# Keys, values and the last element's Wh in tiles of 512 positions, projected block by block

## The chip, the cores and the metric

The kernel runs on one core of a Trainium2 chip. The time is the device time of one execution in microseconds (us); beside it the profile gives the span from the first to the last instruction. TensorE (PE) multiplies matrices, VectorE (DVE), ScalarE (ACT) and GpSimd (POOL) work on tiles, and SyncE (SP) issues all the DMAs of this kernel, in program order.

## What is computed

Two layers on a graph of N = 2048 nodes, for a batch of 8 elements with 256 features:

```python
# layer 0: attention of 4 heads (D = 64), softmax within chunks of 256 keys, the chunks summed
q, k, v = (x @ W.T + b for W, b in ((Wq, bq), (Wk, bk), (Wv, bv)))
s = clip(q @ k.T / 8, -10, 10); s = where(adj == 0, -10, s)
ctx = sum over chunks j of softmax(s[:, chunk j]) @ v[chunk j]
h = layernorm(x + layernorm(ctx @ Wo.T + bo + x) * gamma + beta)
# layer 1: graph attention
Wh = h @ W; si = Wh @ a[:256]; sj = Wh @ a[256:]
e = where(adj > 0 or i == j, leaky_relu(si[:, None] + sj[None, :], 0.2), -inf)
out = layernorm(h + elu(softmax(e) @ Wh))
```

`adj` is the same for all elements. All arithmetic is float32.

## The kernel before

**Order by hand.** The order of instructions is the program's own; each engine takes its instructions in that order, and the framework adds the waits. The main loop (from L749) runs over J, the pairs of key tiles: 8 elements x 4 query blocks of 512 (`IB`) x 8 chunks of 256 keys, and each J has two halves. A half is a *beat*: one tile of 128 keys against 512 queries, all heads. There are 512 beats with scores, 64 per element and 16 per query block; `2 * total` in the code is beat 512. After it a drain loop (L868) runs beats without scores.

**A beat.** `begin_beat` advances layer 1's pipeline of an earlier element (`low` on ScalarE L611, `leaky` L615 and `edges` L620 on VectorE, `weights` on ScalarE L624). Then come the scores (L775, TensorE), the clip and mask in one VectorE instruction (L785), the exponentials (L788, ScalarE), and the products of the exponentials of the previous J with the values and with ones (L801, TensorE). Sums go out to a DMA (`dc`, L817), are inverted (L823), stored (`rd`, L825) and spread over the partitions (`r`, L829); two beats later `un` is scaled (L836) and added to `ctxT` by GpSimd (L837). `end_beat` does layer 1's products with Wh (L643, and L658 for the last element), then advances generators one step each: `ahead` (the preludes of layer 1) and `fins` (the end of layer 0 for a query block, `fin`; of layer 1, `fin1`; and the making of masks). After beat 512 `fins` goes first.

**Keys and values.** They lie in one tile each per element: `kT` (2 x 2048 per partition) and `v` (16 x 256), both from a pool of one buffer (`one`). `make_kT` projects four blocks of 512 (L252, evicted by ScalarE L253) in one go: for element 0 before the main loop, for the others at the last beat of the element before, behind `make_qT`. `make_v` (L270, L277) follows after the first two beats of an element. Both load the transposed input, `xT` tiles of 512 KB from a pool of four, anew for keys and for values (`xT_k`, `xT_v`); the query block has its own load (`xT_q`). Accumulators of projections, ctx products, transposes and Wh share the PSUM pool `ps_m`, two buffers with the tag `m`.

**Masks of element 0.** The first mask block (`first_m0`) is made in four pieces of VectorE L154 and ScalarE L161 ahead of the loop; `masks_made` makes the other one of each pair and the later blocks, `far_made` the row masks `far`, both during element 0.

**Layer 1's prelude.** `prelude` multiplies h with W (`wh_block`, L370, L371), takes the key columns (`key_columns`, L380 to L382), turns them into a row on every partition (`key_rows`, L388 to L393), and finds each query's largest allowed sum with 32 maxima over half rows (`half_max`, L412), for which `far` is loaded into two buffers `fb`. `last_prelude` does it for element 7 when no scores are left to hide it: its `wh` takes the place of `kT`, and `sj_row` that of `v`, both from beat 512 on. The first half rows need Wh blocks 0 and 1; three first-half maxima are issued in each beat until `hT`, the transposed h of the last query block, is there (made by `fin`, L352 to L359, at beat 520: output projection L331 with its add L338 and statistics at 515, normalization L303 at 516, GpSimd L343 and L344 at 517, statistics at 518, normalization at 519). Then follow the last Wh block and the second half rows. Eight rows of `far` are held whole in the places of the exponentials.

The parts that the diff touches, and what calls them:

## Time and profile before

| | us |
|---|---|
| median of 3 runs | 4439.85 (4435.65 to 4445.19) |
| the profiled execution, its own time | 4440.12 |
| its span | 4438.3 |
| TensorE busy | 4076.7 (92%) |
| VectorE busy | 3412.6 (77%) |
| ScalarE busy | 2604.1 (59%) |
| GpSimd busy | 1782.7 (40%) |
| one key-tile score instruction of VectorE (L785), mean | 1.221 |
| one exponential (L788), mean | 1.022 |

A profile line names the line of the kernel, the engine, the operation, the tile that is written and those that are read (`sc<-qT,kT`), the form, and how many; in a timeline the first two numbers are the start and the length in us, and brackets hold the idle time of the engine just before, with what ended it. "PEld" is TensorE's loading of weights, which overlaps its matmuls. A projected block of keys is 8 matmul rows in the trace, of values 16. Of the whole span, the profile's chain of waits is only followed back for a part; the stages are therefore read from the busy time of each engine in a stretch.

### The profile page before, as it was taken

What the parts mean: (1) busy time and instruction counts of PE and PEld (TensorE: products, weight loads), DVE (VectorE), ACT (ScalarE), POOL (GpSimd) and SP (SyncE); (2) the same over time, 40 slices, a digit from 0 to 9 for tenths busy, and PEclk for the clock granted to TensorE, in tenths of its full rate; (3) what the DMA queues carried; (4) which work ended last, traced back from release to release, by engine and by line L of the source; (5) the groups of instructions that cost most, each with busy time, mean ns of one, the idle gap of its engine ahead of it and who ended that gap; (6) DMA issues with size and microseconds to landing.
All of it is one profiled execution on the core that took longest, in us unless ns stands there. A gap on an engine that the chain in (4) does not pass through costs nothing. (4 is left out here: it accounts for less than half of the span.)

```text
span 4438.3 us, 61328 instructions
## 1 busy us (share of the span) xinstructions
PE 4076.7 (92%) x23053; PEld 1913.9 (43%) x23053; DVE 3412.6 (77%) x4530; ACT 2604.1 (59%) x3878; POOL 1782.7 (40%) x906
## 2 busy tenths in 40 slices
PE   7888999999899999999989999999989999899767
PEld 3222334444344443445434453444534445344455
DVE  4776468985799758996599966898569975898786
ACT  4666456665556655666556655566555665566455
POOL 0222224553255523554334543455325543355521
PEclk9999999999999999999999999999999999999889
DMA  4555333322322323223333223332332232332321
GB/s 145 165 161 154 93 104 102 96 89 82 102 84 90 100 67 113 86 79 95 93 92 101 82 75 106 97 105 74 90 105 83 92 96 75 109 94 78 117 79 53
DMA packets 266601, 432.93 MB, mean 98 GB/s; under 512 B 85952, under 2 KB 121024, under 8 KB 265408
## 3 DMA queue, kind: packets, MB, share of 16 engines
q1 hardware_dynamic: 266304, 429.01, 31.5%
q8 instruction: 181, 2.97, 0.3%
q14 instruction: 116, 0.95, 0.1%
HBM read 357.96 MB, written 68.88 MB: 96 GB/s over the span
## 5 line engine op out<-in xcount | busy, mean ns | idle before, releaser
L788 ACT ACTIVATE e<-sc 128x1024 f32<-128x1024 f32 x1024 | 1037.3, 1022 | 1144.9 <-DVE sc L785 1100.5
L785 DVE SCALAR_TENSOR_TENSOR sc<-sc,mk 128x1024 f32<-128x1024 f32 x1024 | 1205.5, 1221 | 519.6 <-PE sc L775 287.1
L775 PE MATMUL sc<-qT,kT 64*128 64x512 f32 x4096 | 1063.6, 633 | 108.6 <-ACT e L788 105.9
L837 POOL TENSOR_TENSOR ctxT<-ctxT,un 128x1024 f32<-128x1024 f32 x224 | 564.9, 2522 | 1173.6 <-DVE un L836 1068.1
L801 PE MATMUL u<-e,v 128*32 128x512 f32 x8192 | 982.5, 597 | 0.0
L643 PE MATMUL us<-wh,w 128*128 128x256 f32 x3584 | 875.9, 393 | 74.3 <-ACT w L624 56.6
L643 PEld LDWEIGHTS us<-wh,w 128*128 128x128 f32 x3584 | 663.9, 192 | 416.6 <-ACT w L624 110.6
L633 POOL TENSOR_TENSOR acc<-acc,w 128x512 f32<-128x512 f32 x392 | 607.8, 1551 | 528.6 <-ACT w L624 512.7
L775 PEld LDWEIGHTS sc<-qT,kT 64*128 64x128 f32 x4096 | 347.5, 189 | 631.3 <-ACT e L788 310.8
L615 DVE SCALAR_TENSOR_TENSOR w<-ab,sj,w 128x512 f32<-128x512 f32 x512 | 587.6, 1168 | 15.4 <-ACT w L611 15.3
L801 PEld LDWEIGHTS u<-e,v 128*32 128x32 f32 x8192 | 240.3, 110 | 660.2 <-issue 539.6
L620 DVE TENSOR_TENSOR w<-w,mk 128x512 f32<-128x512 f32 x512 | 467.8, 934 | 42.9 <-DMA mk<-mask 40.0
L801 PE MATMUL u<-e,ones 128*32 128x512 f32 x4096 | 497.8, 604 | 0.0
L412 DVE CUSTOM_DVE_ANT_0 fb<-sj_row,fb 128x1024 bf16<-128x1024 f32 x240 | 383.8, 1608 | 2.4 <-DMA fb<-far 2.4
L611 ACT ACTIVATE w<-ab,sj 128x512 f32<-128x512 f32 x512 | 353.7, 716 | 18.0 <-PE us L658 11.9
L624 ACT ACTIVATE w<-w 128x512 f32<-128x512 f32 x512 | 310.5, 631 | 66.3 <-DVE w L620 64.9
L836 DVE TENSOR_TENSOR un<-un,r 128x1024 f32<-128x1024 f32 x224 | 278.8, 1244 | 88.2 <-DMA r<-rd 72.7
L809 ACT COPY un<-u 128x512 f32<-128x512 f32 x512 | 300.6, 587 | 54.8 <-PE u L801 52.9
L801 PEld LDWEIGHTS u<-e,ones 128*32 128x32 f32 x4096 | 107.7, 110 | 357.3 <-issue 315.7
L823 DVE RECIPROCAL dc<-dc 128x16 f32<-128x16 f32 x256 | 64.1, 250 | 180.3 <-DMA dc<-ds 155.2
L573 POOL TENSOR_TENSOR hx<-hx,hr 128x1024 f32<-128x1024 f32 x32 | 91.6, 2862 | 177.8 <-DVE hx L572 177.8
L658 PE MATMUL us<-wh,w 128*128 128x257 f32 x512 | 127.6, 412 | 28.8 <-ACT w L624 28.8
(100 smaller groups left out, 3163.1 us busy)
## 6 DMA issues: line engine op xcount, KB each, us to landing
r<-rd SPq DMA_DIRECT2D x256, 256.0 KB
mk<-mask SPq DMA_DIRECT2D x120, 512.0 KB
fb<-far SPq DMA_DIRECT2D x240, 256.0 KB
xT_k<-in_xT_dram SPq DMA_DIRECT2D x32, 512.0 KB
raw<-in_adjT_dram SPq DMA_DIRECT2D x32, 512.0 KB
xT_q<-in_xT_dram SPq DMA_DIRECT2D x32, 512.0 KB
rawf<-in_adj_dram SPq DMA_DIRECT2D x32, 512.0 KB
xT_v<-in_xT_dram SPq DMA_DIRECT2D x32, 512.0 KB
```

The costliest lines, as they stand in the source:

```text
L412: nc.vector.tensor_tensor_reduce(out=fb, in0=sj_row[:, ts(hf, HN)], in1=fb, scale=1.0, scalar=2 * FAR * 0.999, op0=ALU.add, op1=ALU.max, a ...
L611: nc.scalar.activation(self.w, k["ab"][:, 1, :], AF.Identity, bias=k["sj"][:, 1, c : c + 1])
L615: nc.vector.scalar_tensor_tensor(self.w, k["ab"][:, 0, :], k["sj"][:, 0, c : c + 1], self.w, ALU.add, ALU.max)
L620: nc.vector.tensor_tensor(self.w, self.w, self.k["mks"][self.c // HT][:, self.c % HT, :], ALU.min)
L624: nc.scalar.activation(self.w, self.w, AF.Exp)
L633: nc.gpsimd.tensor_add(k["acc"], k["acc"], self.w)
L643: nc.tensor.matmul(k["us"][:, t, :], self.w[:, ts(t, P)], k["wh"][:, c, 0:F], start=(first and t % 2 == 0), stop=last, skip_group_check=True,)
L775: nc.tensor.matmul(sc[:, h, :], kT[h * D : (h + 1) * D, hp, ts(c, P)], qT[h * D : (h + 1) * D, hp, :], start=True, stop=True,)
L785: nc.vector.scalar_tensor_tensor(scs[hp], scs[hp], -CLIP, cap, ALU.max, ALU.min)
L788: nc.scalar.activation(e, scs[hp], AF.Exp)
L801: nc.tensor.matmul(m[h * DH : (h + 1) * DH, :], prev["v"][:, pc, f0 : f0 + DH] if part < 2 else ones[:, 0:DH], prev["es"][2 * i + h // 2][ ...
L837: nc.gpsimd.tensor_add(p["ctxT"], p["ctxT"], p["un"])
```

## The change

Keys and values of an element become four tiles each, with buffers of their own (`kT0` to `kT3`, `v0` to `v3`). A generator, `projections`, projects block n of keys and, a beat or two later, block n of values, from the same `xT` tile. For element b > 0 that is at beats 4n + 4 and 4n + 5 of the last query block of element b - 1, when the old block n has had its last use. In element 0 key block 0 is made ahead of the loop, and the query block from the same `xT`; value block 0 at beat 0; key blocks at beats 2, 6, 10, and value blocks at 4, 8, 12. The first mask block is made one piece ahead of the loop and three in beats 0 to 2; the first loads are reordered to suit.

In the last element Wh block n (n = 0 to 2) goes into the place of `kT` n, at beats 502, 506 and 510, and its key columns with it; the first half row goes into the place of `v0`. One first-half maximum is issued per beat from beat 511 on, with every row mask from the two `fb` buffers; the second-half row masks, two rows to a tile, are the ones held in the places of the exponentials. Layer 1 reads Wh as a list of four tiles.

```diff
@@ -122,7 +122,7 @@
         return t
 
     WT = {"k": load_w("k", WkT)}
-    first_xT = [xT_tile(0, ib, "k") for ib in range(2)]
+    xT_kv = {(0, 0): xT_tile(0, 0, "k")}
     WT["q"] = load_w("q", WqT)
     bk_c = load_c("bk_c", bk)
     bq_c = load_c("bq_c", bq)

...
@@ -176,13 +176,16 @@
                     blocks0[ib, hf] = m0
                 m1 = two.tile([P, HT, IB], I8, tag="mask1", name=f"mb1_{ib}_{hf}")
                 for i in range(HT // 2 + 2):
-                    if i < HT // 2 and not first:
+                    if first:
+                        if 0 < i < HT // 2:
+                            make_mask(0, m0, raw, ib, hf, 2 * i, 2)
+                    elif i < HT // 2:
                         load_raw(raw, ib, hf, 2 * i, 2)
                     if i >= 2:
                         if not first:
                             make_mask(0, m0, raw, ib, hf, 2 * i - 4, 2)
                         make_mask(1, m1, raw, ib, hf, 2 * i - 4, 2)
-                    if i >= 2 or not first:
+                    if i or not first:
                         yield
                 nc.sync.dma_start(out=mask[0][ib, hf], in_=m0)
                 nc.sync.dma_start(out=mask[1][ib, hf], in_=m1)

...
@@ -204,10 +207,12 @@
                 yield
 
     first_raw = one.tile([P, HT, IB], I32, tag="wh", name="raw0_0")
-    for i in range(0, HT, 2):
-        load_raw(first_raw, 0, 0, i, 2)
-    first_xT.append(xT_tile(0, 2, "k"))
+    load_raw(first_raw, 0, 0, 0, 2)
     WT["v"] = load_w("v", WvT)
+    load_raw(first_raw, 0, 0, 2, 2)
+    xT_kv[0, 1] = xT_tile(0, 1, "k")
+    load_raw(first_raw, 0, 0, 4, 2)
+    load_raw(first_raw, 0, 0, 6, 2)
     WT["o"] = load_w("o", WoT)
     bv_c = load_c("bv_c", bv)
 

...
@@ -252,32 +257,52 @@
                 nc.tensor.matmul(pm, WT[name][:, k, ts(o, P)], xt[:, k, :], start=(k == 0), stop=(k == KC - 1))
             nc.scalar.activation(dst[:, o, :], pm, AF.Identity, bias=bias[:, o : o + 1], scale=scale)
 
-    def make_kT(b, tiles):
-        kT = one.tile([P, NPAIR, N], F32, tag="kT", name=f"kT{b}")
-        for ib in range(NIB):
-            proj_T(kT[:, :, ts(ib, IB)], "k", tiles[ib], bk_c, 1.0, f"k{b}_{ib}")
-            if len(tiles) < NIB:
-                tiles.append(xT_tile(b, len(tiles), "k"))
-        return kT
-
-    def make_v(b, tiles):
-        v = one.tile([P, NT, F], F32, tag="v", name=f"v{b}")
-        for ib in range(NIB):
-            for t2 in range(TPB // 2):
-                pv = ps_m.tile([P, 2, F], F32, tag="m", name=f"pv{b}_{ib}_{t2}")
-                for j in range(2):
-                    for k in range(KC):
-                        nc.tensor.matmul(
-                            pv[:, j, :],
-                            tiles[ib][:, k, ts(2 * t2 + j, P)],
-                            WT["v"][:, k, :],
-                            start=(k == 0),
-                            stop=(k == KC - 1),
-                        )
-                nc.scalar.copy(v[:, ib * TPB + 2 * t2 : ib * TPB + 2 * t2 + 2, :], pv)
-            if len(tiles) < NIB:
-                tiles.append(xT_tile(b, len(tiles), "v"))
-        return v
+
+
+    kTs = [[None] * NIB for _ in range(B)]
+    vs = [[None] * NIB for _ in range(B)]
+
+    def make_kT(b, n):
+        kTs[b][n] = one.tile([P, NPAIR, IB], F32, tag=f"kT{n}", name=f"kT{b}_{n}")
+        proj_T(kTs[b][n], "k", xT_kv[b, n], bk_c, 1.0, f"k{b}_{n}")
+
+    def make_v(b, n):
+        xt = xT_kv.pop((b, n))
+        vs[b][n] = one.tile([P, TPB, F], F32, tag=f"v{n}", name=f"v{b}_{n}")
+        for t2 in range(TPB // 2):
+            pv = ps_m.tile([P, 2, F], F32, tag="m", name=f"pv{b}_{n}_{t2}")
+            for j in range(2):
+                for k in range(KC):
+                    nc.tensor.matmul(
+                        pv[:, j, :],
+                        xt[:, k, ts(2 * t2 + j, P)],
+                        WT["v"][:, k, :],
+                        start=(k == 0),
+                        stop=(k == KC - 1),
+                    )
+            nc.scalar.copy(vs[b][n][:, ts(t2, 2), :], pv)
+
+    def projections():
+
+
+        for b in range(B):
+            first = (b * NIB - 1) * 2 * NCH
+            for n in range(NIB):
+
+
+                k_beat = 4 * n - 2 if b == 0 else first + 4 * n + 4
+                while beat < k_beat - 2:
+                    yield
+                if (b, n) not in xT_kv:
+                    xT_kv[b, n] = xT_tile(b, n, "k")
+                while beat < k_beat:
+                    yield
+                if (b, n) != (0, 0):
+                    make_kT(b, n)
+                    yield
+                while beat < k_beat + 2 and b == 0:
+                    yield
+                make_v(b, n)
 
     def make_qT(b, ib, xt):
         qT = one.tile([P, NPAIR, IB], F32, tag="qT", name=f"qT{b}_{ib}")

...
@@ -493,48 +517,54 @@
 
 
         st = states[b]
-        while beat < 2 * total - 4 or fin_near[b] < NIB - 1:
-            yield
-        hts = [load_hT(b, ib) for ib in range(NIB - 1)]
-        while beat < 2 * total:
-            yield
-        wh = one.tile([P, NT, F + 2], F32, tag="kT", name=f"wh{b}")
-        sj = two.tile([P, 3, NT], F32, tag="sj", name=f"sj{b}")
-        wh_block(b, wh, hts[0], 0)
-        yield
-        wh_block(b, wh, hts[1], 1)
+        wh, rows = [None] * NIB, [None] * 2
         halves = [slice(0, HT), slice(HT, NT)]
-        key_columns(wh, sj, halves[0])
-        yield
-        sj_row = one.tile([P, N], F32, tag="v", name=f"sj_row{b}")
-        key_rows(b, sj, sj_row, halves[0])
-        wh_block(b, wh, hts[2], 2)
-
-        held = []
-        for it in range(HT):
-            fr = eight.tile([P, N], BF16, tag="e", name=f"far{b}_{it}")
-            nc.sync.dma_start(out=fr.rearrange("p (n w) -> p n w", n=2), in_=far[it].rearrange("n p w -> p n w"))
-            held.append(fr)
-        fbs, fb_load = far_loads(b, [(it, hf) for hf in range(2) for it in range(HT, NT)])
-        yield
+        sj = None
+        for ib in range(NIB - 1):
+
+            while fin_near[b] <= ib or beat < 2 * total - 12 + 4 * ib:
+                yield
+            ht = load_hT(b, ib)
+            yield
+            yield
+            wh[ib] = one.tile([P, TPB, F + 2], F32, tag=f"kT{ib}", name=f"wh{b}_{ib}")
+            wh_block(b, wh[ib], ht, ib)
+            if sj is None:
+                sj = two.tile([P, 3, NT], F32, tag="sj", name=f"sj{b}")
+            key_columns(wh[ib], sj, slice(ib * TPB, (ib + 1) * TPB))
+            nc.vector.memset(wh[ib][:, :, F : F + 1], 1.0)
+            yield
+            if ib == 1:
+                rows[0] = one.tile([P, HN], F32, tag="v0", name=f"sj_row{b}_0")
+                key_rows(b, sj, rows[0], halves[0])
+                fbs, fb_load = far_loads(b, [(it, 0) for it in range(NT)])
         m2 = one.tile([P, NIB, 2, TPB], F32, tag="m2l", name=f"m2{b}")
+        firsts = list(range(NT))
+        held = None
 
         def half(it, hf):
-            fb = held[it][:, ts(hf, HN)] if it < HT else fbs.pop(0)
-            half_max(sj_row, fb, hf, m2[:, it // TPB, hf, it % TPB : it % TPB + 1])
-            if it >= HT:
+            fb = fbs.pop(0) if hf == 0 else held[it // 2][:, ts(it % 2, HN)]
+            half_max(rows[hf], fb, m2[:, it // TPB, hf, it % TPB : it % TPB + 1])
+            if hf == 0:
                 fb_load()
 
-        firsts = list(range(NT))
         while "hT" not in st:
-            for it in firsts[:3]:
-                half(it, 0)
-            firsts = firsts[3:]
-            yield
-        wh_block(b, wh, st["hT"], NIB - 1)
-        key_columns(wh, sj, halves[1])
-        nc.vector.memset(wh[:, :, F : F + 1], 1.0)
-        key_rows(b, sj, sj_row, halves[1])
+            if firsts:
+                half(firsts.pop(0), 0)
+
+            if beat >= 2 * total + 2 and held is None:
+                held = []
+                for n in range(HT):
+                    fr = eight.tile([P, 2, HN], BF16, tag="e", name=f"far{b}_{n}")
+                    nc.sync.dma_start(out=fr, in_=far[2 * n : 2 * n + 2, 1].rearrange("t p w -> p t w"))
+                    held.append(fr.rearrange("p t w -> p (t w)"))
+            yield
+        wh[-1] = one.tile([P, TPB, F + 2], F32, tag=f"kT{NIB - 1}", name=f"wh{b}_{NIB - 1}")
+        wh_block(b, wh[-1], st["hT"], NIB - 1)
+        key_columns(wh[-1], sj, slice(NT - TPB, NT))
+        nc.vector.memset(wh[-1][:, :, F : F + 1], 1.0)
+        rows[1] = one.tile([P, HN], F32, tag="v1", name=f"sj_row{b}_1")
+        key_rows(b, sj, rows[1], halves[1])
         st["wh"], st["sj"] = wh, sj
         yield
         while firsts:

...
@@ -735,23 +765,22 @@
 
     first_m0 = two.tile([P, HT, IB], I8, tag="mask0", name="mk0_0_0_0")
     blocks0 = {(0, 0): first_m0}
-    kT = make_kT(0, first_xT)
-    for i in range(0, HT, 2):
-        make_mask(0, first_m0, first_raw, 0, 0, i, 2)
-    qT = make_qT(0, 0, xT_tile(0, 0, "q"))
+    make_kT(0, 0)
+    make_mask(0, first_m0, first_raw, 0, 0, 0, 2)
+    qT = make_qT(0, 0, xT_kv[0, 0])
+    fins.append(projections())
     fins.append(weights_made())
     fins.append(masks_made())
     fins.append(far_made())
 
     prev = None
-    v = None
     mk0 = {}
     for J in range(total + 1):
         b, ib, j = J // (NIB * NCH), J // NCH % NIB, J % NCH
         live = J < total
         if live and j == 0:
             ctxT = one.tile([P, 2, IB], F32, tag="ctx", name=f"ctxT{b}_{ib}")
-        cur = {"b": b, "ib": ib, "j": j, "es": [], "ctxT": ctxT, "v": None, "name": f"{b}_{ib}_{j}"}
+        cur = {"b": b, "ib": ib, "j": j, "es": [], "ctxT": ctxT, "v": vs[min(b, B - 1)], "name": f"{b}_{ib}_{j}"}
         for half in range(2):
             c = 2 * j + half
             if live:

...
@@ -845,23 +874,11 @@
             end_beat()
             if half == 1:
 
-
                 if live and j == NCH - 2 and J + 2 < total:
                     nb, nib = (b, ib + 1) if ib + 1 < NIB else (b + 1, 0)
                     xq = xT_tile(nb, nib, "q")
-                    if nb != b:
-                        tiles = [xT_tile(nb, i, "k") for i in range(2)]
                 if live and j == NCH - 1 and J + 1 < total:
                     qT = make_qT(nb, nib, xq)
-                    if nb != b:
-                        kT = make_kT(nb, tiles)
-                        tiles_v = [xT_tile(nb, i, "v") for i in range(3)]
-                if live and J % (NIB * NCH) == 0:
-                    if b == 0:
-                        tiles_v = [xT_tile(0, i, "v") for i in range(3)]
-                    v = make_v(b, tiles_v)
-                if live:
-                    cur["v"] = v
             beat += 1
         prev = cur if live else None
 
...
```

What is left out passes the lists `kTs`, `vs` and Wh tiles where one tile was passed (L775, L801, L643, L658), and gives `half_max` and `key_rows` the half row itself.

## The prediction

> **What bounds the kernel now.** First the page's busy times and the answer by stage: start, length, then busy time (and instructions) of PE, PEld, DVE, ACT, POOL, then granted TensorE clock, DMA share and GB/s.
>
> ```profile
> PE 4076.7 (92%) x23053; PEld 1913.9 (43%) x23053; DVE 3412.6 (77%) x4530; ACT 2604.1 (59%) x3878; POOL 1782.7 (40%) x906
> ...
> 40.00:157.20 117.20, 96.21 (x550) 36.24 (x552) 73.15 (x105) 69.84 (x83) 11.78 (x5) 0.93 0.40 125
> 373.40:497.20 123.80, 103.50 (x584) 33.66 (x580) 73.87 (x104) 64.79 (x85) 35.05 (x15) 0.96 0.47 146
> ...
> 3617.50:3654.50 37.00, 37.00 (x157) 17.58 (x159) 17.61 (x29) 21.42 (x32) 13.24 (x9) 1.00 0.53 157
> ...
> 4023.60:4142.50 118.90, 116.05 (x709) 52.50 (x702) 101.57 (x130) 75.80 (x113) 63.37 (x33) 1.00 0.24 75
> ...
> 4164.60:4209.60 45.00, 20.06 (x73) 15.38 (x72) 39.48 (x61) 13.64 (x24) 19.60 (x10) 0.70 0.43 159
> ```
>
> Three regimes. In element 0 (the rows at 40 and 373 us) TensorE idles 20 of 117 and 20 of 124 us, and no engine is full. From element 1 to the last score TensorE is full: 116.05 of 118.90 us in the last query block, 37.00 of 37.00 around an element boundary. In the tail (4164 to 4210) VectorE is full, 39.48 of 45 us, and TensorE waits. So moved TensorE work is worth something only if it lands in the first or third regime.
>
> Next TensorE in order of time (start, length, operation, and in brackets the idle time before it): the prologue, then the boundary of elements 5 and 6, with VectorE's row there.
>
> ```profile
> 5.72 9.05 PE L252 MATMUL pk<-xT_k,WT_k 128*128 128x512 f32 x16 [5.72 <-DMA xT_k<-in_xT_dram]
> ...
> 24.95 6.24 PE L252 MATMUL pk<-xT_k,WT_k 128*128 128x512 f32 x8 [5.50 <-DMA xT_k<-in_xT_dram]
> ...
> 36.69 3.57 PE L775 MATMUL sc<-qT,kT 64*128 64x512 f32 x8 [2.07 <-ACT qT L253]
> ...
> 63.11 1.99 PE L775 MATMUL sc<-qT,kT 64*128 64x512 f32 x8
> ```
> ```profile
> 3111.39 13.90 PE L252 MATMUL pk<-xT_k,WT_k 128*128 128x512 f32 x32
> ...
> 3139.96 13.98 PE L270 MATMUL pv<-WT_v,xT_v 128*128 128x256 f32 x64
> ```
> ```profile
> 3126.46 2.36 DVE L785 SCALAR_TENSOR_TENSOR sc<-sc,mk 128x1024 f32<-128x1024 f32 x2 [18.15 <-ACT kT L253]
> ```
>
> The first scores start at 36.69 us, and those of beat 2 at 63.11, after all four key and value blocks. At the boundary the 27.9 us of projections have no TensorE gap inside them; it is VectorE that starves, 18.15 us.
>
> **Step A, start of element 0.** After the change only key block 0 and query block 0 precede the scores. From 5.72 us: the first five of eight weight loads come 0.85 apart, later ones 0.43 (timeline of the weight loads: 9.27, 9.89, 10.32), so key block 0 ends near 11.3, the query block 8 x 0.43 later at 14.7, its eviction (0.69 plus a hand-over) at 15.4: 21.3 us earlier than 36.69. The scores of beats 0 and 1 and value block 0 (16 x 0.215 = 3.4) follow; weight preparation (four of 0.42) and a mask piece (0.68) lie before beat 1's clip (2.36). I put beat 2's scores at 25, against 63.11: **-38**. Into beats 2 to 12 then go back three key and three value blocks, 6 x 3.43 = **+20.6**.
>
> How much of that is hidden? The waits between 64 and 500 us (who waited, for whom: us in all, times, longest):
>
> ```profile
> DVE un L836 <- DMA r<-rd: 35.2, 13, 5.3
> ...
> PE pq L252 <- ACT un L809: 9.0, 4, 4.6
> ```
>
> VectorE stands in order at L836 until the reciprocal sums come back through DRAM; these stalls leave TensorE gaps of 6.86 us after beat 7's products and 5.03 around beat 13. A projection in front of them is free, as the round trip runs on meanwhile: 10 of 11.9 us taken, **-10**. Against that, an inserted projection needs an accumulator that ScalarE must first empty: the query projections, the nearest row, paid 9.0/4 = 2.25 us each in element 0. One in that range often coincides with a wait for the exponentials that the scores would have had anyway, so between 0 and 2.25 I take 0.7: 6 x 0.7 = **+4**. The three mask pieces (ScalarE 3 x 1.15, VectorE 3 x 0.68) lay in the prologue and now precede clips: **+2** of 5.5 shown, the rest beside TensorE. The second mask block is also made a beat later, right ahead of beat 8's clip; that is at most 2.5 us once, in the ends. A = -38 + 20.6 - 10 + 4 + 2 = **-21** (ends -12, -32). The loads of xT blocks 2 and 3 now stand in SP's queue ahead of rd and r; each is 512 KB, but the four xT_v and the query's xT are gone from before beat 0, so I book nothing, worst +2 each.
>
> **Step B, element 0 to 1.** Eight blocks, 27.5 us, go from the two full bursts at the boundary into beats 52 to 65. TensorE idles 15.4 us in 383 to 464 (81.00 - 65.58), again from the r stalls. Blocks go in at beats 52, 53, 56, 57, 60, 61, and the gaps at beats 52 to 55 and 58 take about 8; insertion costs 8 x 0.5 = 4. B = **-4** (-12, +4).
>
> **Step C, six further boundaries.** Here a rule of the Trainium skill differs from the row. "Perfetto Trace Analysis", Optimization Strategy, says that a kernel with several regimes can gain by interleaving them; by that rule VectorE's 18.15 + 13.42 us of starving per boundary are to be won, 6 x 27 = up to 160 us. The row says otherwise: the stretch that receives the blocks is as full as the one that loses them. In 1964 to 2048, beats 4 to 15 of such a query block's 16, TensorE is busy 82.59 of 84.00 us, and most of the idle 1.4 is in its first beat. Twenty-seven microseconds put there cost 27. The row decides: -0.5 each, **-3** (ends -10, if every gap fills; +15, if each of 8 insertions waits 0.3 us: in element 6 the query projections wait 2.5 us in four, 0.6 each, and not all of it would be new). The added waits: ScalarE's eviction of a key block waits for TensorE at the end of the beat, with the layer-1 exponentials, `low` and the score exponentials queued behind it; TensorE waits for them next, but has scores (1.9) and ctx products (1.9 to 3.6) in between. The 33 loads less (32 xT_v, one xT_q) cost nothing either way at a DMA share of 0.2 to 0.3.
>
> **Step D, the tail.** (1) Three Wh blocks, 3 x 3.65 = 11 us, go from beats 512 to 514 to beats 502, 506, 510, where TensorE idles 2.85 of 118.9: +11. Their three hT loads go out one at a time (beats 500, 504, 508) and land two beats ahead. VectorE's key columns wait there for the Wh copies, as they do now for 7.86 us; behind them stand the reciprocal and the next clip, whose scores are behind Wh on TensorE too, so nothing is added. Without them the output projection, at 4164.65 now, waits for ctx and layer-1 products (9.5 us from 4142.6) and for the round trip, r and POOL's sum (about 4150): 4152, -12.6. Together **-2**. (2) From there to hT VectorE runs in order; its rows, with the load that the maxima waited for:
>
> ```profile
> 4177.17 0.16 DVE L301 SCALAR_TENSOR_TENSOR nmr_a<-mv_a,rstd_a 128x4 f32<-128x4 f32 x1
> ...
> 4192.08 0.42 DVE L292 BATCH_NORM_STATS2 st_b<-y 128x6 f32<-128x256 f32 x1
> ...
> 4202.23 0.15 DVE L301 SCALAR_TENSOR_TENSOR nmr_b<-mv_b,rstd_b 128x4 f32<-128x4 f32 x1
> ```
> ```profile
> 4195.73 2.69 DMA fb<-far
> ...
> 4204.97 3.17 DMA fb<-far
> ```
>
> Three maxima of 1.15 to 3.3 us stand in each beat; after the change one. nmr_a comes 2.3 earlier (two maxima); nmr_a to st_b is 14.9 now and at least ACT 2.1 + POOL 2.79 + 2.68 = 7.6; st_b to nmr_b is 10.1 and would be about 6 (stats 2.3, POOL 2.0, one maximum, one layer-1 step). -2.3 - 7.3 - 4 = -13.6, booked **-12**. (3) What is late next: only 9 of the 16 first-half maxima are done when hT arrives, where 15 are done now, and seven stand ahead of the second half. Two tiles have landed; the other five share two buffers, so each takes (1.15 + 3)/2 = 2.1: 2.3 + 10.4 = 12.7 us against 3.0 now (one maximum and the rest of the wait for sj_row): **+9**. D = -2 - 12 + 9 = **-5** (-18, +8). The eight held loads of 512 KB stay at beat 514.
>
> **Sum.** -21 - 4 - 3 - 5 = -33 against the profiled execution's 4440.12 us, which is 0.3 from the median of 4439.85: **4407 us**, 0.75% less.
>
> **A rule that speaks against step A.** "TensorE: Matmul & The Clock Gate", Why this matters for your kernels, asks for no TensorE gaps over about 3 us, since the clock then falls to half. Cutting a solid burst into pieces between waiting scores would, by it, leave beats 0 to 3 cold: the prologue's own stretch from 20 to 40 us, with two such gaps, was granted 0.75, which is 5 us lost. By the rule A would be -16. But the new start is 9 us of unbroken key and query matmuls, and the blocks fill gaps of an element that runs at 0.93 already; I book 0 and keep the 5 in A's end.
>
> **The rivals.**
> R1, transfers pace the start anyway: 35.2 us of waits for r speak for it, since an earlier start meets rawf and mask loads sooner; the DMA share of 0.00 between 40 and 60 us speaks against. A falls to -6: 4422.
> R2, the freed boundaries pay: if each boundary returns 6 of its 31 starved us, 36 more: 4371. Against it stands 37.00 of 37.00.
> R3, slower: every insertion stops TensorE until ScalarE has emptied the accumulators. For 62 blocks (6 + 8 + 48) it decides from (33 + 9)/62 = 0.68 us a block above what is booked; at 1 us the time is 4407 + 62 = 4469. For it: the pq row's 2.25 us in element 0; against: in the full stretches that wait mostly vanishes.
> R4, no change: A is right but the seven late maxima run behind their loads at 3 us each and B and C lose their upper ends (+8 +4 +8 for D, B, C): 4407 + 13 + 8 + 11 = 4439.
>
> **How the numbers follow.** Forecast 0.55 (own range 4393 to 4420), R1 0.17, R2 0.16, R3 0.05, R4 0.07. Leaving out half of R2, R3 and most of R4 gives 4380 to 4427. Beyond 0.2% (8.9 us, about what these measurements can tell) faster are the forecast, R2 and nearly all of R1, 0.88; same is R4 and a little of R1, 0.07; slower R3, 0.05.
>
> **What would show it.** A: first scores near 15 us, beat 2's near 25, element 0's first query block over near 136 (157 now), with the gaps at beats 7 and 13 gone. B and C: no pk or pv run over 4 us after the start; query blocks 3 some 25 us longer and blocks 0 as much shorter, the pair unchanged; a longer pair means R3. D: hT's evictions some 14 us sooner after the output projection, then seven maxima waiting for fb. The forecast is wrong if the scores of beat 2 come after 32 us, or if the waits of pk and pv for ScalarE sum to over 40 us.

## The result, and the profile after

The changed kernel takes 4424.01 us, median of 7 runs (4414.97 to 4428.54), where the kernel before took 4439.53 beside it: a ratio of 0.9962 with a 95% interval from 0.9951 to 0.9974. It is faster, by 16.4 us (the mean of two measured ratios, 0.9962 and 0.9964 in e5), half of the 33 that the prediction booked. The profiled execution took 4424.23 us, its span 4422.4.

The busy times on the page are nearly those of before (TensorE 4076.7, VectorE 3412.6): no work went away, it moved.

```profile
PE 4070.1 (92%) x23053; PEld 1907.1 (43%) x23053; DVE 3408.3 (77%) x4539; ACT 2599.2 (59%) x3878; POOL 1771.9 (40%) x906
```

The answer by stage of the changed kernel follows, with the columns as before. Its rows are element 0's first and last query block, beats 4 to 15 of a middle element's last query block, the last element's last sixteen beats, and the two parts of the tail: output projection to hT, and hT to the first query rows.

```profile
17.00:130.20 113.20, 103.76 (x571) 38.47 (x573) 73.56 (x104) 74.88 (x90) 11.90 (x6) 0.97 0.48 149
346.90:463.40 116.50, 107.88 (x624) 40.70 (x620) 71.75 (x104) 66.63 (x89) 28.82 (x13) 0.99 0.46 140
1924.00:2008.00 84.00, 82.55 (x450) 42.16 (x449) 58.88 (x68) 55.28 (x87) 36.66 (x20) 1.00 0.26 77
3989.40:4117.00 127.60, 120.70 (x716) 57.81 (x705) 96.62 (x136) 75.55 (x120) 57.00 (x30) 1.00 0.23 72
4146.40:4179.30 32.90, 17.70 (x72) 14.27 (x71) 26.42 (x44) 13.11 (x24) 20.16 (x11) 0.79 0.56 198
4179.30:4208.70 29.40, 6.47 (x29) 4.54 (x27) 20.39 (x45) 5.98 (x13) 3.48 (x3) 0.69 0.25 81
```

TensorE's idle time in element 0's two rows is 9.4 and 8.6 us, where it was 21.0 and 20.3. The middle stretch is as full as it was (82.55 of 84 us). The sixteen last beats took 110.4 us before (4023.6 to 4134.0) and take 127.6 now, and TensorE idles for 6.9 us of them where it idled for 2.85.

TensorE in order of time, start of the changed kernel:

```profile
5.73 5.29 PE L257 MATMUL pk<-xT_k,WT_k 128*128 128x512 f32 x8 [5.73 <-DMA xT_k<-in_xT_dram]
10.86 3.60 PE L257 MATMUL pq<-xT_k,WT_q 128*128 128x512 f32 x8
14.39 1.99 PE L804 MATMUL sc<-qT,kT 64*128 64x512 f32 x8
...
23.55 2.26 PE L804 MATMUL sc<-qT,kT 64*128 64x512 f32 x8 [1.60 <-ACT e L817]
```

The scores of beat 0 come at 14.39 and those of beat 2 at 23.55 (before 36.69 and 63.11). The two traces laid side by side by beat (the start of ScalarE's first exponential of its scores) show where the difference sits:

| stretch | before to after, us | predicted |
|---|---|---|
| start to beat 16 (step A) | -27.0 | -21 |
| beat 16 to element 1's second query block (step B) | -12.0 | -4 |
| from there to beat 496, six boundaries (step C) | +4.8 | -3 |
| beat 496 to the end (step D) | +18.3 | -5 |
| sum | -15.9 | -33 |

Up to beat 496 it is 34 us ahead, more than the 28 that were forecast for A, B and C. Then it gives back 18. VectorE at two of the Wh blocks, and TensorE's wait for the first query rows:

```profile
4080.72 0.17 DVE L406 COPY sj<-wh 128x4 f32<-128x4 f32 x1 [6.32 <-ACT wh L397]
...
4113.42 0.17 DVE L406 COPY sj<-wh 128x4 f32<-128x4 f32 x1 [7.49 <-ACT wh L397]
...
4193.64 1.23 DVE L436 CUSTOM_DVE_ANT_0 fb<-sj_row,fb 128x1024 bf16<-128x1024 f32 x1 [4.26 <-DMA fb<-far]
```
```profile
4208.63 0.38 PE L459 MATMUL pab<-ident,m 128*8 128x128 f32 x1 [21.14 <-DVE m L455]
```

The question for the experiments is thus the end: step D, and within it which part.

### The profile page after: what moved, and what is told of

Its sections match the earlier page's. It is cut to its first block, busy times and chain, and to the rows that moved or that the text cites. A ratio compares the mean times of both kernels' runs of the same rounds, so it can differ in the third digit from the quotient of the medians.

```text
span 4422.4 us, 61235 instructions
## 1 busy us (share of the span) xinstructions
PE 4070.1 (92%) x23053; PEld 1907.1 (43%) x23053; DVE 3408.3 (77%) x4539; ACT 2599.2 (59%) x3878; POOL 1771.9 (40%) x906
## 3 DMA queue, kind: packets, MB, share of 16 engines
q1 hardware_dynamic: 257328, 411.71, 30.6%
## 5 line engine op out<-in xcount | busy, mean ns | idle before, releaser
L645 DVE SCALAR_TENSOR_TENSOR w<-ab,sj,w 128x512 f32<-128x512 f32 x512 | 578.5, 1150 | 16.3 <-ACT w L641 16.1
L688 PE MATMUL us<-wh,w 128*128 128x257 f32 x512 | 127.1, 410 | 30.6 <-ACT w L654 30.6
```

Source lines behind the costliest of these rows:

```text
L645: nc.vector.scalar_tensor_tensor(self.w, k["ab"][:, 0, :], k["sj"][:, 0, c : c + 1], self.w, ALU.add, ALU.max)
```

## Experiments

Each kernel is the changed kernel with the edit shown, unless said. Line numbers in an experiment's profile are those of its own code. Ratios are to the kernel before on the same chip; the changed kernel's own is 0.9962. Chips differ: the kernel before takes 4430.88 us on that of e1 to e4 and 4438.10 on that of e5 to e8, so a time in us is not compared across them. Because executions of one kernel differ by several us before beat 480, the end is also read from the trace in five stretches, from the exponential's start at one beat to the next mark: beats 480 to 511; beat 511 to the output projection (po); to hT's eviction; to the transpose of the first query rows (pab); and to the end.

| kernel | 480-511 | to po | to hT | to pab | to the end | ratio, 95% interval |
|---|---|---|---|---|---|---|
| before | 235.1 | 30.6 | 44.3 | 16.4 | 213.0 | 1 |
| changed | 253.5 | 29.4 | 32.9 | 29.4 | 213.8 | 0.9962 (0.9951-0.9974) |
| e5 changed, again | 253.9 | 27.3 | 33.8 | 29.0 | 213.3 | 0.9964 (0.9950-0.9978) |
| e1 old end | 234.6 | 30.2 | 44.7 | 16.3 | 213.5 | 0.9942 (0.9927-0.9957) |
| e2 new end alone | 254.0 | 27.2 | 33.9 | 28.8 | 213.4 | 1.0052 (1.0035-1.0069) |
| e3 columns later | 245.7 | 27.9 | 32.8 | 28.9 | 214.2 | 0.9960 (0.9945-0.9974) |
| e4 maxima from 515 | 252.0 | 25.9 | 33.7 | 36.9 | 214.0 | 0.9990 (0.9981-0.9999) |
| e6 bursts at boundaries | 252.5 | 27.9 | 34.3 | 29.3 | 213.3 | 0.9954 (0.9941-0.9966) |
| e7 element 0 at once | 252.3 | 28.7 | 32.8 | 28.9 | 214.1 | 0.9981 (0.9974-0.9988) |
| e8 end rearranged | 236.1 | 29.7 | 36.3 | 23.7 | 214.0 | 0.9933 (0.9918-0.9947) |
| e9 e8, adds earlier | 237.1 | 28.9 | 35.7 | 23.7 | 213.5 | 0.9935 (0.9921-0.9948) |
| e10 e1, adds earlier | 238.0 | 29.0 | 44.0 | 16.7 | 212.6 | 0.9945 (0.9932-0.9957) |
| e11 e4, adds earlier | 252.6 | 20.4 | 33.9 | 37.0 | 214.0 | 0.9977 (0.9969-0.9985) |
| e12 e9, third Wh later | 236.5 | 25.2 | 39.5 | 23.7 | 213.5 | 0.9939 (0.9926-0.9952) |

**e1: the old end.** `last_prelude` as it was, its tiles renamed (Wh blocks in kT0 to kT3, the two halves of the key row in v0 and v1):

```diff
-            while fin_near[b] <= ib or beat < 2 * total - 12 + 4 * ib:
-                yield
-            ht = load_hT(b, ib)
...
+        while beat < 2 * total:
+            yield
+        block(0, hts[0])
+        yield
+        block(1, hts[1])
...
-            if firsts:
-                half(firsts.pop(0), 0)
+            for it in firsts[:3]:
+                half(it, 0)
```

> The changed kernel with the last element's end as it was before: the three Wh blocks at beats 512, 513 and 514, their key columns and the first-half maxima three in a beat from beat 515, second-half rows 0 to 7 held. Theory (the rewritten end costs 18 us, as the two traces show between beat 496 and the end, and what was won before beat 496, 34 us, doesn't depend on it): 4424 - 18 = 4406 us, 4400 to 4412, with po again about 30 us after beat 511. Rival (the prediction's step D, the rewritten end gains 5): 4429 us. A third (the 18 us come from the keys and values in four tiles and not from the end): 4424 us, no change.

Measured: 4405.83 us, ratio 0.9942. That it meets the 4406 expected is in part the chip's doing: by the ratios the old end is only 8.9 us shorter than the changed kernel, with an interval of some 8 us either way. The trace is sharper. It puts 18.9 us into beats 480 to 511 (253.5 to 234.6); what follows beat 511 sums to 304.7, and to 305.5 in the changed kernel. So in the trace the end costs what the theory says, and the rest of step D comes to nothing; in the times the cost is there, and its size is not settled by this run.

**e2: the new end alone,** in the kernel before. Only the tiles and the end differ from it:

```diff
-        kT = one.tile([P, NPAIR, N], F32, tag="kT", name=f"kT{b}")
+        kT = [one.tile([P, NPAIR, IB], F32, tag=f"kT{ib}", name=f"kT{b}_{ib}") for ib in range(NIB)]
-        v = one.tile([P, NT, F], F32, tag="v", name=f"v{b}")
+        v = [one.tile([P, TPB, F], F32, tag=f"v{ib}", name=f"v{b}_{ib}") for ib in range(NIB)]
```

> The kernel before with keys and values in tiles of 512, but projected in its own bursts at their old places; only the last element's end is the changed kernel's. Theory (the end costs 18 us by itself): 4440 + 18 = 4458 us, 4450 to 4464. Rival (step D of the prediction, -5): 4435 us. Together with the old end in the changed kernel it says whether the two parts add up: both should differ from their base by the same number with opposite signs.

Measured: 4451.85 us, ratio 1.0052: slower, by 23.1 us. With e1 it makes a square: projecting block by block is worth 25.7 us with the old end (0.9942 of 4439.5) and 39.5 with the new one (1.0052 to 0.9963), 33 on average; the new end costs 23.1 without it and 9.3 with it, 16 on average. Each has an interval of 7 to 9 us either way, and the traces' 34 and 18 agree with the means.

**e3: key columns a beat later.**

```diff
             wh_block(b, wh[ib], ht, ib)
+            yield
             key_columns(wh[ib], sj, slice(ib * TPB, (ib + 1) * TPB))
             nc.vector.memset(wh[ib][:, :, F : F + 1], 1.0)
-            yield
             if ib == 1:
+                yield
                 rows[0] = one.tile([P, HN], F32, tag="v0", name=f"sj_row{b}_0")
```

> The changed kernel, with the key columns (three small copies on VectorE) and the column of ones of the Wh blocks of beats 502, 506 and 510 issued one beat after the block's matmuls. Theory (VectorE stands at these copies for 6.3 and 7.5 us while ScalarE has not yet evicted the Wh block, and the next beat's score steps stand behind them): the waits go, beats 502 and 506 lengthen by TensorE's 3.65 us and no longer by 5.6 to 6.8, total 4424 - 6 = 4418 us. Rival (the matmuls themselves are the whole cost, the wait only shows it): 4424 us, within 2.

VectorE in order of time, the same two copies in this kernel:

```profile
4082.01 0.16 DVE L406 COPY sj<-wh 128x4 f32<-128x4 f32 x1
...
4111.83 0.16 DVE L406 COPY sj<-wh 128x4 f32<-128x4 f32 x1
```

No idle time stands before them, and beats 480 to 511 take 245.7 us instead of 253.5. Beat by beat it is the three with a Wh block that change: beat 502 takes 7.1 us in the kernel before, 12.7 in the changed one and 8.9 here; beat 506 takes 8.0, 14.7 and 10.9; beat 510 takes 7.4, 12.7 and 10.9. What stays over the old end's 235 is 10.6 us: three Wh blocks of 3.65, at their full price. The time itself (0.9960) does not resolve the 7.8 us; the trace does.

**e4: maxima from beat 515.**

```diff
-            if firsts:
+            if firsts and beat >= 2 * total + 3:
                 half(firsts.pop(0), 0)
```

> The changed kernel, with the first-half maxima starting at beat 515 instead of 511, still one in a beat. Theory (the maxima of beats 511 to 514 stand in VectorE's queue ahead of the last two contexts' scale, one of them 3.37 us long beside GpSimd): po comes 6 to 8 us sooner after beat 511, 22 instead of 29.4, and four more maxima are left after hT at 1.2 us each, +5 and some waits for their rows: 4424 - 2 = 4422 us, 4418 to 4426. Rival (VectorE had room there, po waits for the transfers of the softmax sums): po at 29 us as now, and 4424 + 6 = 4430 us.

Measured 0.9990, by the ratios 12 us longer than the changed kernel: the theory missed. Its five stretches sum to 562.5 us, only 3.5 and 5.2 more than in the two executions of the changed kernel; the rest of the 12 is not in the end and is not explained. The output projection comes only 1.4 to 3.5 us sooner, while the way from hT to pab grows by 7.5, 1.9 us for each of the four maxima put off. With neither Wh nor a maximum in its way, the output projection still starts 25.9 us after beat 511; VectorE and GpSimd in that stretch of e4:

```profile
4131.24 2.71 DVE L650 TENSOR_TENSOR w<-w,mk 128x512 f32<-128x512 f32 x1
4133.88 4.51 DVE L645 SCALAR_TENSOR_TENSOR w<-ab,sj,w 128x512 f32<-128x512 f32 x2
4138.31 2.34 DVE L650 TENSOR_TENSOR w<-w,mk 128x512 f32<-128x512 f32 x2
4140.58 1.21 DVE L865 TENSOR_TENSOR un<-un,r 128x1024 f32<-128x1024 f32 x1
```
```profile
4128.31 2.35 POOL L347 TENSOR_TENSOR y<-x,bo_bc 128x1024 f32<-128x1024 f32 x1 [3.84 <-PE u L830]
4130.74 2.67 POOL L348 TENSOR_TENSOR x<-x,beta_bc 128x1024 f32<-128x1024 f32 x1
4133.37 2.80 POOL L866 TENSOR_TENSOR ctxT<-ctxT,un 128x1024 f32<-128x1024 f32 x1
```

VectorE has hardly a gap (23.03 of the 25.85 us are busy), its layer-1 steps are about two to four times as long as elsewhere (0.69 and 0.74 us), and GpSimd works beside them (the last section reads these pairs). That gave the theory for e9 to e11.

**e5: the changed kernel again,** no edit, as base for e6 to e8.

> The changed kernel itself once more, so that the other three runs of this call have their base on the same chip: 0.996 of the time before, 0.995 to 0.997.

Measured 0.9964.

**e6: bursts at the six boundaries from element 2 on.**

```diff
-        for b in range(B):
+        for b in range(2):
...
                     qT = make_qT(nb, nib, xq)
+                    if nb != b and nb >= 2:
+                        burst_k(nb, tiles)
+                        tiles_v = [xT_tile(nb, i, "v") for i in range(3)]
+                if live and J % (NIB * NCH) == 0 and b >= 2:
+                    burst_v(b, tiles_v)
```

> The changed kernel, with the keys and values of elements 2 to 7 projected in bursts at the six boundaries, each at its old place and from tiles loaded twice; elements 0 and 1 and the end as changed. The prediction's step C (the boundaries gain 3): 3 us longer than the changed kernel. Reading of the two traces (the last query blocks lengthen by what the first ones shorten, sum +4.8, not told from nothing): within 5 us of it, rather 5 shorter than longer. Rival R2 (the freed boundaries pay): 36 us longer. The Trainium skill's rule on interleaving regimes, taken at its most: up to 160 us longer.

Measured 4418.81 us against e5's 4419.57, ratios 0.9954 and 0.9964: no loss, and R2's 36 us is out. The stage answers for element 4's last query block and element 5's first, of e5 and then of e6:

```profile
2404.40:2558.70 154.30, 149.99 (x832) 77.83 (x825) 117.20 (x154) 96.04 (x149) 73.61 (x40) 1.00 0.26 76
2558.70:2686.20 127.50, 122.80 (x713) 56.94 (x705) 70.57 (x98) 71.19 (x110) 43.00 (x23) 0.99 0.23 71
```
```profile
2410.00:2557.20 147.20, 142.85 (x793) 70.34 (x789) 119.91 (x155) 94.61 (x145) 75.12 (x40) 1.00 0.30 91
2557.20:2692.10 134.90, 129.79 (x751) 64.25 (x745) 71.91 (x98) 73.65 (x115) 43.79 (x23) 0.99 0.23 71
```

The pair takes 281.8 and 282.1 us. All six such pairs sum to 1682.9 us in e5 and 1682.6 in e6 (1681.4 before, 1682.4 changed). VectorE's two long waits are gone with the blocks; in e6 they are there:

```profile
2555.89 2.36 DVE L828 SCALAR_TENSOR_TENSOR sc<-sc,mk 128x1024 f32<-128x1024 f32 x2 [17.14 <-ACT kT L258]
...
2584.55 2.36 DVE L828 SCALAR_TENSOR_TENSOR sc<-sc,mk 128x1024 f32<-128x1024 f32 x2 [13.43 <-ACT w L668]
```

Two waits of 30.6 us together come and go, and the time stays, because TensorE is busy 96 to 97% of both stretches in both kernels. VectorE does not even idle less without them: 94.0 us of the pair in e5 and 90.3 in e6. The same idle time is only cut into shorter pieces, 7.33 us the longest in e5.

**e7: element 0's blocks one after the other.**

```diff
-                k_beat = 4 * n - 2 if b == 0 else first + 4 * n + 4
+                k_beat = (n + 1 if n else -2) if b == 0 else first + 4 * n + 4
...
-                while beat < k_beat + 2 and b == 0:
-                    yield
```

> The changed kernel, with element 0's second to fourth key and value blocks projected at beats 2 to 5, one after the other, and not at beats 2, 4, 6, 8, 10 and 12; their x tiles are loaded two at beat 0. Theory (step A: the start comes early either way, and what more is won is that the later blocks fill TensorE's gaps in beats 7 to 14, where it waited for transfers of the softmax sums): the gaps come back, 7 to 10 us longer than the changed kernel. Rival (the gain is the early start alone): no change, within 3 us. A third (six blocks at once starve VectorE and ScalarE as the old burst did): over 12 us longer.

Measured 0.9981 against e5's 0.9964: 7.5 us longer by the ratios, 9.7 by the medians, as the theory has it. By the traces element 0's second query block starts 7.4 us later than in the changed kernel, 8.9 later than in e5. Beats 6 to 15, of the changed kernel and then of e7:

```profile
59.30:130.20 70.90, 67.05 (x384) 24.03 (x380) 46.39 (x62) 48.19 (x59) 11.90 (x6) 0.98 0.59 182
```
```profile
73.40:137.60 64.20, 53.00 (x332) 15.20 (x328) 46.10 (x62) 43.34 (x51) 11.75 (x5) 0.97 0.56 169
```

TensorE idles 3.9 us of the one and 11.2 of the other: 7.3 us of gaps that the later blocks fill.

**e8: the end rearranged,** Wh blocks after beat 511 and most maxima late but with their rows held:

```diff
+        for row in range(0, NT, 2):
+            hold(eight, "e", row, 0)
+        yield
+        hold(one, "v2", 0, 1)
+        hold(one, "v3", 2, 1)
...
+        share = [0, 2, 2, 1, 2]
         while "hT" not in st:
-            if firsts:
-                half(firsts.pop(0), 0)
+            for it in range(share.pop(0) if share else 1):
+                half(firsts.pop(0), 0)
```

> The changed kernel with another end: Wh blocks at beats 512 to 514 as before, the key columns of the first two a beat later than the second's matmuls (no VectorE wait), all sixteen first halves and the first four second halves held in tiles that are free by then, and the first-half maxima 0, 2, 2, 1 and 2 in beats 515 to 519 and the other nine after hT. Theory (a Wh block costs its matmuls where TensorE is full, before beat 512, and nearly nothing after; a maximum that VectorE does before hT costs 1.2 to 1.5 us, and the nine later ones 1.2 each less what the wait for the second half's key rows covers): beat 511 to the output projection 28, from there to hT 34, to the first query rows 24, to the end 213.5: 299.5 instead of 305.5, and beat 480 to 511 at 235 instead of 253.5: 24 us shorter than the changed kernel, 18 to 28. Rival (the order of the maxima moves nothing, only the Wh blocks count): 19 shorter, as with the old end.

Measured 4408.82 us, 0.9933: shorter than e5 by 10.8 us (medians) or 13.8 (ratios), where the theory had 24 and the rival 19. The five stretches sum to 17.5 us less than e5's; this execution reaches beat 480 8.7 us later, in code that is the same, and why is not known. The Wh blocks bring 17.8 us in beats 480 to 511. The order of the maxima brings next to nothing: po to pab sums to 60.0 us, against 61.0 with the old end (fifteen maxima before hT) and 62.3 in the changed kernel (nine). Here seven come before hT: eight fewer than with the old end shorten the way to hT by 8.4 us and lengthen the way from there to pab by 7.4. The rival was right on that point.

**e9 and e10: GpSimd's two additions two beats earlier,** in e8 and in e1. The same edit in both:

```diff
-                            if p["j"] == NCH - 3:
+                            last = (p["b"], p["ib"]) == (B - 1, NIB - 1)
+                            if p["j"] == (NCH - 4 if last else NCH - 3):
...
         nc.gpsimd.tensor_add(xt, xt, bc_rows(beta_bc))
         yield
+        if (b, ib) == (B - 1, NIB - 1):
+            yield
+            yield
```

> The kernel of e8_end_rearranged, with GpSimd's two additions for the very last normalization (y and x, 2.35 and 2.67 us) two beats earlier, at beat 510 and not 512, and nothing else. Theory (after beat 511 the way to the output projection is VectorE's and GpSimd's, not TensorE's: layer-1 steps of 0.69 and 0.74 us take 2.4 to 4.5 us on VectorE while GpSimd does these additions, and the context's addition stands in GpSimd's queue behind them; that is why Wh's 11 us of matmuls there cost so little): VectorE's steps of beats 512 and 513 return to under 2 us, and the output projection starts 25 us after beat 511 and no longer 29.7, 4 to 5 us off the total: ratio to the kernel before 0.992. Rival (TensorE with the three Wh blocks, or the transfers of the softmax sums, set it): 29 to 30 us as now, 0.993.

> The same two additions two beats earlier, in the kernel of e1_old_tail. Theory: output projection 26 us after beat 511 and no longer 30.2, ratio to the kernel before 0.993 where e1 had 0.994. Rival: 30 us, no change; key columns wait there 8 us for ScalarE, which can hide what VectorE gets back.

Measured 0.9935 and 0.9945, no change, and the output projection at 28.9 and 29.0 us (29.7 and 30.2 without the edit): the theory missed in both. VectorE's steps did not return to under 2 us either (in e9 2.87 and 2.74 are the longest, each beside one of GpSimd's additions to the context). The next guess was that there are two ways, and TensorE's is the other. TensorE in e9, before the output projection:

```profile
4115.85 3.65 PE L399 MATMUL pw<-W_aug,hTl 128*128 128x258 f32 x16
4120.50 1.99 PE L684 MATMUL us<-wh,w 128*128 128x256 f32 x8 [0.99 <-ACT w L665]
4122.33 3.65 PE L399 MATMUL pw<-W_aug,hTl 128*128 128x258 f32 x16
4125.82 0.27 PE L417 MATMUL psj<-ident,sj 128*8 128x128 f32 x1
4127.20 3.72 PE L684 MATMUL us<-wh,w 128*128 128x256 f32 x16 [1.11 <-ACT w L665]
4130.76 3.62 PE L359 MATMUL po<-WT_o,ctxT 128*128 128x256 f32 x16
```

TensorE is busy for 26.8 of those 28.9 us; in e4, without the Wh blocks, for 19.7 of 25.9.

**e11: neither Wh, nor maxima, nor the additions there** (e4 with the edit of e9).

> The kernel of e4_maxima_from_515 (no Wh block and no maximum between beat 511 and the output projection) with GpSimd's two additions at beat 510. It leaves VectorE's and GpSimd's layer-1 steps and contexts alone in that stretch. Theory (TensorE with Wh, and VectorE with GpSimd, are two ways of about the same length there, so that taking one away shows the other): with both shortened the output projection starts 21 to 22 us after beat 511, where it was 25.9 with the additions in the stretch, and 29 with Wh in it and the additions out; total about 4 us below e4's, a ratio of 0.998. Rival (the softmax sums' transfers set it): 25 to 26 us, no change.

Measured: output projection 20.4 us after beat 511, ratio 0.9977, as the theory has it (a little sooner than its 21 to 22). With e4 and the ends that keep Wh there, this is a square of its own:

| output projection after beat 511, us | additions in | additions out |
|---|---|---|
| Wh in | 29.7 to 30.6 (e8, e1, before) | 28.9 and 29.0 (e9, e10) |
| Wh out, no maxima | 25.9 (e4) | 20.4 (e11) |

Wh alone brings some 5 us, the additions alone about 1, both together 10. (The upper row also has key columns in that stretch, which e4 and e11 have ahead of it.) The corner of e4 holds one thing more, TensorE's clock, which the next section reads.

**e12: the third Wh block behind the output projection** (e9's kernel).

```diff
-        block(2, hts[2])
         rows[0] = one.tile([P, HN], F32, tag="v0", name=f"sj_row{b}_0")
...
         while "hT" not in st:
+            if beat == 2 * total + 4:
+                block(2, hts[2])
```

> The kernel of e9_adds_earlier, with the third Wh block at beat 516, behind the output projection, and not at 514. Theory (TensorE's queue before the output projection, 3.65 us of it this block, has become the later way there): output projection 25 to 26 us after beat 511, no longer 28.9, and TensorE has room for the block while VectorE and GpSimd normalize: 3 us less in all, ratio to the kernel before 0.992 to 0.993. Rival (the block is only put from one full place into another, its evictions in ScalarE's queue ahead of the normalization): no change, 0.9935.

Measured 0.9939: the output projection comes at 25.2 us, as expected, and hT 39.5 after it and no longer 35.7. The rival holds: the 3.7 us are given back at once, the block's second half stands for ScalarE's eviction of the first:

```profile
4137.26 1.91 PE L399 MATMUL pw<-W_aug,hTl 128*128 128x258 f32 x8
4143.96 3.81 PE L399 MATMUL pw<-W_aug,hTl 128*128 128x258 f32 x8 [4.79 <-ACT wh L400]
```

The ratios of e1, e8, e9, e10 and e12 (0.9933 to 0.9945) are not told apart by their intervals, and all lie below the changed kernel's 0.9962, though the intervals of all but e8 and e9 overlap its own. Of these the changed kernel with the old end (e1) is the simplest, and the one to keep.

## Why the prediction was half right

The direction and the mechanism in element 0 held; step D failed. The time, 4424, lies in the range that was given (4380 to 4427), near its end, and outside the forecast's own 4393 to 4420. That it still lies in the range is partly luck: A and B brought 14 us more than booked, which hid more than half of D's miss of 23. D itself, +18, lies outside its ends of -18 and +8.

**Step A, right, a little small.** The early start came as worked out (scores at 14.39 for 15, beat 2's at 23.55 for 25). Beat 2's scores came 39.6 us sooner, where 38 was booked. From there to beat 16 the blocks gave back 12.6, where 16.6 was booked: TensorE's idle time fell from 16.0 to 7.8 us, by 8.2, and the terms for it (-10, +4, +2) netted only -4. By e7's trace 7.3 of the 8.2 are the later blocks in the gaps. The waits of key and value blocks for ScalarE, of the changed kernel, whole run:

```profile
PE pk L257 <- ACT ds L844: 3.9, 4, 1.5
...
PE pv L276 <- ACT un L838: 1.4, 1, 1.4
PE pk L257 <- ACT un L838: 1.2, 6, 0.2
PE pv L276 <- ACT ds L844: 0.8, 1, 0.8
```

That is 7.3 us for 62 blocks, but not evenly: the six of element 0 waited 2.4 us (booked 4), the eight that follow 3.7 (booked 4), and the other 48, in the full stretches, 1.2. So the booked sizes were near; what was booked too small is the idle time that the blocks fill. R3 needed 0.68 us a block above what was booked; it got none.

The clock-gate rule was rightly left at 0 here: the first query block was granted 0.97, and 0.93 before, and from 5.7 to 40 us the clock was 1.00. The gaps in that query block are at most 2.2 us, so the rule's case of over 3 us did not arise. (Of the two gaps that the prediction counts between 20 and 40 us of the kernel before, only one is over 3 us: 5.50 and 2.07.) It arose in the tail, where the prediction did not look for it; see step D(1).

**Step B, -12 instead of -4:** TensorE's idle time in element 0's last query block fell by 11.7 us (20.3 to 8.6), the 3.7 us of added waits already taken off, where 8 less 4 was booked. The 4 was right; the gaps filled were nearly twice the 8.

**Step C, right in kind.** The six pairs of query blocks take 1.0 us longer than before, and with the bursts put back (e6) 0.3 us less than in e5. The other 3.8 of the trace's +4.8 lie in query blocks where nothing was changed. The row (TensorE full on both sides) decided rightly against what the prediction drew from the Trainium skill, "Perfetto Trace Analysis", Optimization Strategy. That page says only that interleaving regimes may improve performance; here it brought nothing, since the stretch that receives the work had no room on the engine that is moved. (The 6 x 27 was a slip too: the two waits named sum to 31.6 us.) One detail of "what would show it" was miscounted: a last query block grows by 7 to 8 us and not by 25, since only three of the four blocks go into it and the key burst of before already stood at its end.

**Step D(1) is the step that failed.** It said that Wh at beats 502, 506 and 510 costs 11 and that "nothing is added" by VectorE's wait for it, and that Wh's absence brings the output projection 12.6 us sooner: -2 together. Measured: beats 480 to 511 +18.4, and beat 511 to the output projection -1.2 (-3.3 in the second execution); some +16 together.
- Of the 18.4, 10.6 are Wh's matmuls in full stretches, as booked. The other 7.8 is the wait that was costed at nothing: e3 takes it away. Behind the three copies stood the next beat's clip and the layer-1 steps, and with them TensorE's next scores; the 3.65 us of Wh were no cover for 5.2 to 7.5 us of waiting. The kernel before had one such wait, as long, but behind its last scores:

```profile
4153.96 0.17 DVE L380 COPY sj<-wh 128x8 f32<-128x8 f32 x1 [7.86 <-ACT wh L371]
```

- The 12.6 were taken as though TensorE alone held the output projection. Without Wh and maxima it gains 4.7 (e4, 25.9 against 30.6), and 8.6 once GpSimd's additions are out too (e11 against e9 and e10): VectorE and GpSimd formed a second way, 25.9 us long, beside TensorE's 29 to 30. The estimate of 4152 left out their layer-1 steps there. The maxima at beats 511 to 514 took back another 1.4 to 3.5.
- The second way also slows TensorE. Its matmuls ahead of the output projection, in the kernel before, then twice in the changed one, with the changed kernel's stage answer for the last of these (its clock is the third figure from the end):

```profile
4161.09 3.72 PE L643 MATMUL us<-wh,w 128*128 128x256 f32 x16 [0.99 <-ACT w L624]
```
```profile
4132.54 3.54 PE L673 MATMUL us<-wh,w 128*128 128x256 f32 x8 [4.60 <-ACT w L654]
4139.77 6.76 PE L673 MATMUL us<-wh,w 128*128 128x256 f32 x16 [3.68 <-ACT w L654]
...
4139.70:4146.40 6.70, 6.63 (x17) 5.34 (x18) 5.62 (x5) 2.25 (x5) 4.38 (x2) 0.53 0.63 207
```

With Wh gone, TensorE stands still for 4.60 and 3.68 us, and after each gap its granted clock is 0.55 and 0.53; the same sixteen matmuls take 6.76 us and not 3.72, and the output projection stands right behind them. In e4 (gaps of 3.83 and 2.32) they take 5.14, in e11 (1.57 and 1.96, clock 1.00) 3.72. This is the case of the clock-gate rule that the prediction weighed for step A alone. It is the smaller part: GpSimd's last addition to the context, which the output projection needs, ends 1.1 us before that in e4 and 1.6 us before it in the changed kernel, so that without the lower clock no more than that would be won.

**Steps D(2) and D(3), mechanism right, the second mis-sized.** Two maxima fewer per beat: -11.4, booked -12. The seven late ones: +13.0, booked +9; VectorE stood 7.7 us for their loads (4.26, 1.73, 0.24 and 1.45). Together +1.6 and not -3. In e8 the late maxima run without waits at 1.15 us each, and still nothing is won: there a maximum moved across hT costs behind it 0.9 us, nearly the 1.05 that it saves ahead of it.

**The rivals.** R1's 4422 is near the time measured, but not for its reason: the start came early, transfers did not pace it. R4 had the seven maxima behind their loads right in kind, 4.26 us the longest of their waits, but at 3 us each; the way from hT to pab grew by 13.0 for the seven, 1.9 each. R2 and R3 are out by e6 and by the waits above. Neither of the two signs named for a wrong forecast came (beat 2's scores after 32 us, over 40 us of pk and pv waits): both watched A to C, and the miss was in D.

Added up by the trace, the miss of 17 us is D's 23, less the 6 and 8 that A and B did better, plus C's 8, of which about half lies where nothing was changed. Left open are why the times show the cost of the end smaller than the traces in e1 and e8, and what makes e4's 12 us.

## What to carry to other kernels

Work that moves off a stretch is worth only what the second-longest way through that stretch leaves: before booking it, list every engine's queue between the same two events, and not the bound engine's alone. Ask also what the emptied engine does in the gaps that it is left with; here TensorE's clock fell in them. An added wait is free only while everything behind it in that engine's queue has longer cover; add up that cover in us, and issue the waiting instruction a step later if it falls short. Fill gaps that a trace shows by name; exchanging work between two stretches that are full on the same engine brought nothing here, however long another engine starved there.

## What the runs showed of the hardware

Not expected, and left out of the estimate: VectorE's steps and GpSimd's take turns. VectorE and GpSimd of the changed kernel, side by side in the stretch before the output projection:

```profile
4126.70 2.38 DVE L645 SCALAR_TENSOR_TENSOR w<-ab,sj,w 128x512 f32<-128x512 f32 x1
4129.12 2.71 DVE L650 TENSOR_TENSOR w<-w,mk 128x512 f32<-128x512 f32 x1
4131.75 3.37 DVE L436 CUSTOM_DVE_ANT_0 fb<-sj_row,fb 128x1024 bf16<-128x1024 f32 x1
```
```profile
4126.18 2.35 POOL L347 TENSOR_TENSOR y<-x,bo_bc 128x1024 f32<-128x1024 f32 x1 [4.14 <-PE u L830]
4128.61 2.67 POOL L348 TENSOR_TENSOR x<-x,beta_bc 128x1024 f32<-128x1024 f32 x1
4131.24 2.79 POOL L866 TENSOR_TENSOR ctxT<-ctxT,un 128x1024 f32<-128x1024 f32 x1
```

These VectorE instructions take 0.74, 0.69 and 1.22 us where GpSimd is idle. Here each is on record from shortly after the start of one of GpSimd's and ends 0.55, 0.55 and 1.09 us after that one's end: 4129.08 after 4128.53, 4131.83 after 4131.28, 4135.12 after 4134.03. So it waits GpSimd's instruction out and then takes nearly its own time, and the wait counts as busy time of VectorE: no idle time shows it. Not every instruction of VectorE waits. The clip of the scores, in the same kernel, beside one of GpSimd's additions:

```profile
4115.73 2.35 DVE L814 SCALAR_TENSOR_TENSOR sc<-sc,mk 128x1024 f32<-128x1024 f32 x2
```
```profile
4115.15 2.88 POOL L866 TENSOR_TENSOR ctxT<-ctxT,un 128x1024 f32<-128x1024 f32 x1 [9.90 <-DVE un L865]
```

Two clips take 2.35 us here, what two take anywhere (1.221 each). Counted over the changed kernel's whole trace, the 551 clips that start during a GpSimd instruction take 1.22 us in the median, as the others do; the 257 leaky steps (L645) that do take 1.75, the others 0.74; the 82 maxima 2.30 and 1.21. The leaky steps, the edges and the maxima read two tiles from SBUF, the on-chip memory that holds the tiles; the clip reads only the mask there, its scores lie in PSUM. "SBUF — State Buffer", SBUF: two separate sides, in the Trainium skill states that rule: the two engines share a port pair, which a VectorE instruction needs if it has two inputs in SBUF (against a GpSimd instruction that reads SBUF) or runs in a mode that uses both ports; whichever starts first holds it for its whole instruction. The rows agree for the two inputs; the other mode no run here shows. In e11 a step beside the context's addition still took 2.72, so moving one addition only moves the place where they meet.
